# Key weights on ScalarE's DMA queue at the beginning of a one-core decoder kernel

## The chip, the core and the metric

The kernel runs on one core of a Trainium2 chip. A core has a matrix engine (PE, with its weight loads shown apart as PEld), a vector engine (DVE), a scalar engine (ACT), a general engine (POOL), and a sync engine (SP) whose queue issues most of the transfers. The engines run side by side; each takes its own instructions strictly in the order in which they stand in its queue, and waits on semaphores for the others. Transfers between memory and the on-chip buffers are carried by 16 DMA engines. The metric is device time in microseconds (us); less is better.

## The reference, cut to what matters

One decoder layer on 4096 tokens of 512 values: a self-attention without softmax, a cross-attention with softmax on a short context, and a feed-forward block with one shared and 32 routed experts. Only the beginning, the self-attention, is touched by the change:

```
x = residual stream, normalised twice (once before, once in the layer, the second with ln_g and ln_b)
q = x in 4 heads of 128        k = w_fc as 2048 rows of 128 (the same for all tokens)
v = w_proj.T as 2048 rows of 128
out = square(relu(q k^T)) v      x1 = normalised x + residual + out
```

So the keys and values are weights: 512 x 512 numbers each, which are loaded once and serve all tokens and heads.

## The kernel before, in words

**Precision.** Products are made in fp32r with each operand split in a high and a low part. `split` (L89) does it: ACT casts the source to the high part (L94, some calls L96 on DVE), then DVE or POOL subtracts it from the source (L97) to give the low part. A product is then three matrix instructions: high with low, low with high, high with high (`three`, L163). In the profile `kwh`, `kwl` are the parts of the keys (from `wfcT`), `vwh`, `vwl` of the values (from `wpT`), `qh`, `ql` of the queries and `ph`, `pl` of the squared scores. Each weight matrix is four tiles of 128 x 512, 256 KB each. Loads pass through `raw`, a pool of six tiles (L56, L106), so a seventh load waits for the split of the first.

**Stage 0.** `stage0` (L222) goes over tokens in t = 0..7, 512 at a time. `prep(t)` (L231) loads four x tiles (L238), takes their statistics on DVE (L243, L244), a reciprocal root by a power on POOL (L249) and a short chain on DVE (L250 to L254, the last writes `ao`), and writes normalised rows `y` on ACT (L264) or, for two of the four tiles of t = 0, on DVE (L262). Then POOL turns the x tiles into what is added to the attention's output (L273) and SP stores them to `x1` (L274). `prep_head(t, h)` (L278) transposes y for one head on PE (L281), applies gain and bias on ACT (L282) and splits the result.

A step of the main loop (L330) is (t, h, kt): three score products into a bank `s` (L349), relu on ACT into `rl` (L353), square on DVE into `p` or back into the bank (L357), split of p. Seven steps later (`LAG`, L225) `av` (L304) multiplies it with the values into `o` (L311). The score banks alternate between two tags of two buffers each, so that a step needs the bank of the step four before it. There are 512 steps.

**The order of the work.** A planner places the instructions of each engine when the kernel is built, by its own estimate of times and by the order of the code; a program then holds one fixed order for each engine. `g.after(...)` (L73) keeps the instructions in its block behind the named ones on the same engine; `later` (L82) gives a lower priority. All loads and stores of the beginning stand in SP's queue: first the four x tiles, the identity matrix for transposes (L1521), four small stores of an initial list (L1525), gain and bias (L228), then the four tiles of `wfcT` and the four of `wpT` (L107), with mask and zero row between them, and then the weights of the next stage, the stores of `x1` rows and the x tiles of t = 1.

At the beginning, `wfcT` is split behind `g.first`, the normalised rows that DVE writes (L290), the low parts by DVE and POOL in turn; `wpT` is split behind the gain-and-bias step of head 1 (L295), all low parts on DVE; the rows for `x1` follow the last key split (L297), and all four heads of t = 0 are prepared before the loop (L293, L294, L299, L300).

Of the kernel before, what the change touches and what calls it, by code (L numbers as in the profile page):

```python
# [11 lines left out]
I32 = mybir.dt.int32  # L12
# [84 lines left out]
    g.low = (lo_engine or g.nc.vector).tensor_tensor(lo, src, f32(hi), A.subtract)  # L97


def split_steps(g, dram, hi, lo, lo_engine=None):  # L100

    for k in range(len(hi)):
        at = 0
        for h, l in zip(hi[k], lo[k]):
            n = h.shape[-1]
            raw = g.raw.tile([128, n], F32, name="raw", tag="raw")  # L106
            g.nc.sync.dma_start(raw[:], dram[k * 128:(k + 1) * 128, at:at + n])  # L107
            split(g, h, l, raw[:], lo_engine)
            at += n
        if at > 256 or k % 2:  # L110
            yield


def weight_steps(g, dram, nk, width, name, lo_engine=None):
    hi, lo = ([[g.piece(name + z)[:] for _ in range(width // 512)] for _ in range(nk)] for z in "hl")
    yield from split_steps(g, dram, hi, lo, lo_engine)
    return hi, lo


# [99 lines left out]

def stage0(g, x, wfcT, wpT, lnT, x1, background, front):  # L222
    nc = g.nc
    NT = T // 512
    LAG = 7  # L225
    gb = g.c.tile([128, 2, 4], F32, name="gb")
    with later(g, 20):
        nc.sync.dma_start(gb[:], lnT)  # L228
    ys, qs = {}, {}

    def prep(t):  # L231

        rows = [slice(t * 512 + s * 128, t * 512 + s * 128 + 128) for s in range(4)]
        xt = [g.tile("G", "xt") for _ in rows]
        for v, r in zip(xt, rows):
            nc.sync.dma_start(v[:], x[r, :])  # L238
        yield
        mv = g.sm.tile([128, 4, 2], F32, name="am", tag="am")  # L240
        for i, v in enumerate(xt):
            s6 = g.small("as", 6)
            nc.vector.bn_stats(s6[:], v[:])  # L243
            nc.vector.bn_aggr(mv[:, i, :], s6[:])  # L244
            yield
        ve, r0, tt, rs, of = (g.small("a" + z, 8) for z in "vptro")
        nc.vector.tensor_scalar(ve[:, 0:4], mv[:, :, 1], EPS, None, A.add)
        nc.vector.tensor_scalar(ve[:, 4:8], mv[:, :, 1], 1.0 + EPS, EPS * EPS, A.mult, A.add)
        power = nc.gpsimd.tensor_tensor(r0[:], ve[:], g.mhalf[:], A.pow)  # L249
        nc.vector.scalar_tensor_tensor(tt[:], r0[:], -0.5, ve[:], A.mult, A.mult)  # L250
        nc.vector.tensor_tensor(tt[:], tt[:], r0[:], A.mult)
        nc.vector.scalar_tensor_tensor(rs[:], tt[:], 1.5, r0[:], A.add, A.mult)
        mean = mv[:, :, 0].unsqueeze(1).to_broadcast([128, 2, 4])
        nc.vector.scalar_tensor_tensor(of[:].rearrange("p (a n) -> p a n", a=2), mean, -1.0,  # L254
                                       rs[:].rearrange("p (a n) -> p a n", a=2), A.mult, A.mult)
        if t > 0:
            yield
        ys[t] = []
        for i, v in enumerate(xt):
            y = g.tile("C", "y")  # L260
            if t == 0 and i % 2:
                g.first = nc.vector.tensor_scalar(y[:], v[:], mv[:, i, 0:1], rs[:, 4 + i:5 + i], A.subtract, A.mult)  # L262
            else:
                nc.scalar.activation(y[:], v[:], AF.Identity, bias=of[:, 4 + i:5 + i], scale=rs[:, 4 + i:5 + i])  # L264
            ys[t].append(y)
            if i % 2:
                yield

        sc = g.small("bv", 4)
        nc.vector.tensor_scalar(sc[:], rs[:, 0:4], 1.0, None, A.add)  # L270
        for i, v in enumerate(xt):
            with g.after(power):
                nc.gpsimd.tensor_scalar(v[:], v[:], sc[:, i:i + 1], of[:, i:i + 1], A.mult, A.add)  # L273
            nc.sync.dma_start(x1[rows[i], :], v[:])  # L274
            if i % 2:
                yield

    def prep_head(t, h):  # L278
        pt = g.bank("P4", "pt")
        for s in range(4):  # L280
            nc.tensor.transpose(pt[:, s * 128:(s + 1) * 128], ys[t][s][:, h * 128:(h + 1) * 128], g.ident)  # L281
        g.q = nc.scalar.activation(pt[:], pt[:], AF.Identity, bias=gb[:, 1, h:h + 1], scale=gb[:, 0, h:h + 1])  # L282
        qh, ql = g.tile("E", "qh", FR), g.tile("F", "ql", FR)
        split(g, qh[:], ql[:], pt[:])
        qs[t, h] = (qh, ql)

    todo = prep(0)
    while 0 not in ys or len(ys[0]) < 4:
        next(todo)
    with g.after(g.first):  # L290
        kw = run(weight_steps(g, wfcT, 4, 512, "kw", cycle((nc.vector, nc.gpsimd))))
    low = g.low
    prep_head(0, 0)  # L293
    prep_head(0, 1)  # L294
    with g.after(g.q):  # L295
        vw = run(weight_steps(g, wpT, 4, 512, "vw"))
    with g.after(low):  # L297
        run(todo)
    prep_head(0, 2)  # L299
    prep_head(0, 3)  # L300

    P, oT, cur = {}, {}, {}

    def av(t, h, kt):  # L304
        p = P.pop((t, h, kt))
        if kt == 0:
            cur["o"] = g.bank("P3", "o")
        o = cur["o"]
        j, rb = divmod(kt, 4)
        for n, (w, y) in enumerate(three(([part(v, rb, j) for v in vw], p))):  # L310
            nc.tensor.matmul(o[:], w, y[:], start=kt == 0 and n == 0, stop=kt == 15 and n == 2)  # L311
        if kt < 15:
            return
        oT[h] = g.tile("D", "oT")
        nc.scalar.copy(oT[h][:], o[:])
        if h < 3:
            return
        for s in range(4):
            rows = x1[t * 512 + s * 128:t * 512 + s * 128 + 128, :]
            b = g.tile("IJ"[s % 2] if t < NT - 1 else "G", "b")  # L320
            nc.sync.dma_start(b[:], rows)
            pt = g.bank("P4", "pt")
            for hh in range(4):
                nc.tensor.transpose(pt[:, hh * 128:(hh + 1) * 128], oT[hh][:, s * 128:(s + 1) * 128], g.ident)
            nc.vector.tensor_tensor(b[:], pt[:], b[:], A.add)
            nc.sync.dma_start(rows, b[:])

    steps = [(t, h, kt) for t in range(NT) for h in range(4) for kt in range(16)]
    marks = []
    for i, (t, h, kt) in enumerate(steps):  # L330
        if h == 0 and kt == 2 and t + 1 < NT:
            todo = prep(t + 1)
            next(todo)
        if t + 1 == NT and h == 0 and kt == 14:
            todo = front
        if (t + 1 < NT and (h > 0 or kt > 6) or h > 0) and kt % 2:
            with g.after(*marks):
                next(todo, None)
        if (h > 0 if t > 0 else h > 1) and kt % 8 == 6 or t > 0 and h == 0 and kt == 14:
            with g.after(*marks):  # L340
                next(background, None)
        if h > 0 and t + 1 < NT and kt == 12:
            prep_head(t + 1, h - 1)
        if h == 0 and t > 0 and kt == 8:
            prep_head(t, 3)
        s = g.bank(("P1", "P2")[kt % 2], "s")
        j, rb = divmod(kt, 4)
        for n, (w, y) in enumerate(three(([part(k, j, rb) for k in kw], qs[t, h]))):
            nc.tensor.matmul(s[:], w, y[:], start=n == 0, stop=n == 2)  # L349
        if i >= LAG:  # L350
            av(*steps[i - LAG])
        r = g.tile("K", "rl")
        m0 = nc.scalar.activation(r[:], s[:], AF.Relu)  # L353

        apart = i % 8 in (1, 3, 5, 6, 7)
        p = g.tile("H", "p") if apart else s
        m1 = nc.vector.tensor_tensor(p[:], s[:], r[:], A.mult)  # L357
        marks = [m0, m1]
        ph, pl = g.tile("A", "ph", FR), g.tile("B", "pl", FR)
        split(g, ph[:], pl[:], p[:], nc.gpsimd if apart else None, nc.vector if i % 8 == 2 else None)  # L360
        P[t, h, kt] = (ph, pl)
    run(background)
    g.marks = marks
    for st in steps[len(steps) - LAG:]:
        av(*st)
# [1128 lines left out]
def build(tc, I, out):  # L1494
    from contextlib import ExitStack
    nc = tc.nc
    with ExitStack() as outer:
# [15 lines left out]
        with ExitStack() as inner:  # L1513
# [5 lines left out]
            idx = g.c.tile([128, NB], I32, name="idx")  # L1519
            with later(g, 20):  # L1520
                nc.sync.dma_start(ident[:], I["ident"])  # L1521
                empty = g.tile("A", "empty", I32, (128, NBLK))
                nc.gpsimd.memset(empty[:], T)
                for v in lists:
                    nc.sync.dma_start(v[:], empty[:])  # L1525
            g.pairs = Pairs(g, I["sgu"], wS)
            front = {}
            stage0(g, I["x"], I["wfcT"], I["wpT"], I["lnT"], x1,
                   context_steps(g, I["ctxT"], I["wk"], I["wv"], I["wq"], I["wo"], kst, vst),
                   first_rows(g, x1, I["mask"], front))  # L1530
            zero = g.c.tile([128, 4], F32, name="zero")
            nc.gpsimd.memset(zero[:], 0.0)
            nc.sync.dma_start(xs[T:T + 1, :].rearrange("o (p k) -> (o p) k", p=128), zero[:])
# [45 lines left out]
```

## Time and profile before

| | us |
|---|---|
| median of 3 runs | 2693.14 |
| lowest and highest run | 2693.03, 2693.76 |
| profiled execution, its own time | 2691.72 |
| its span, first to last instruction | 2689.9 |
| PE busy | 2631.0 (98%) |
| DVE busy | 2056.8 (76%) |
| ACT busy | 1872.3 (70%) |
| POOL busy | 1205.9 (45%) |

A page of the profile names instructions by line, engine, operation, and `out<-in` by the program's tile names. A timeline row has the start and the length in us, then the instruction, how many of them, and in brackets the engine's idle time before it and what ended that. Windows give each engine's busy time in a stretch. The granted clock of PE is 1.00 in all the windows shown. Of the first 22 us, PE is idle until 11.38, waits until 15.47 for the first product, and until 21.87 for the fifth step's products.

### The profile page before, as it was taken

What the parts mean: (1) busy time and instruction counts of PE and PEld (TensorE: products, weight loads), DVE (VectorE), ACT (ScalarE), POOL (GpSimd) and SP (SyncE); (2) the same over time, 40 slices, a digit from 0 to 9 for tenths busy, and PEclk for the clock granted to TensorE, in tenths of its full rate; (3) what the DMA queues carried; (4) which work ended last, traced back from release to release, by engine and by line L of the source; (5) the groups of instructions that cost most, each with busy time, mean ns of one, the idle gap of its engine ahead of it and who ended that gap; (6) DMA issues with size and microseconds to landing.
All of it is one profiled execution on the core that took longest, in us unless ns stands there. A gap on an engine that the chain in (4) does not pass through costs nothing. (4 is left out here: it accounts for less than half of the span.)

```text
span 2689.9 us, 47615 instructions
## 1 busy us (share of the span) xinstructions
PE 2631.0 (98%) x14592; PEld 2266.3 (84%) x14593; DVE 2056.8 (76%) x4569; ACT 1872.3 (70%) x4155; POOL 1205.9 (45%) x972
## 2 busy tenths in 40 slices
PE   7999999999999999999999998999999999999998
PEld 5888877877789999998988877878989898888886
DVE  7777777777778888898876795674776777778985
ACT  7887787788778777887874332343676767677885
POOL 5765676777654444444446568321122221212221
PEclk9999999999999999999999999999999999999999
DMA  4112112233120324333259656763898899999994
GB/s 154 62 64 95 56 60 91 94 103 104 40 80 18 106 93 136 126 127 126 95 183 365 212 179 202 233 209 111 267 289 275 281 305 293 302 282 290 326 323 140
DMA packets 282289, 463.72 MB, mean 172 GB/s; under 512 B 34512, under 2 KB 85712, under 8 KB 282032
## 3 DMA queue, kind: packets, MB, share of 16 engines
q1 hardware_dynamic: 267344, 433.50, 47.5%
q0 software_dynamic: 14688, 27.17, 4.9%
q8 instruction: 115, 1.88, 0.3%
q14 instruction: 142, 1.16, 0.1%
HBM read 359.58 MB, written 102.93 MB: 172 GB/s over the span
## 5 line engine op out<-in xcount | busy, mean ns | idle before, releaser
L97 DVE TENSOR_TENSOR rl<-raw,rh 128x512 fp32r<-128x512 f32 x768 | 488.8, 685 | 83.7 <-ACT rh L94 58.8
L94 ACT CAST rh<-raw 128x512 fp32r<-128x512 f32 x768 | 437.8, 621 | 135.9 <-DMA raw<-in_rg 85.5
L97 POOL TENSOR_TENSOR pl<-p,ph 128x512 fp32r<-128x512 f32 x320 | 410.8, 1296 | 233.1 <-ACT ph L94 202.8
L353 ACT ACTIVATE rl<-s 128x512 f32<-128x512 f32 x512 | 293.9, 605 | 42.9 <-PE s L349 33.5
L1350 POOL DMA_INDIRECT out_dram<-v,idx x46 | 111.5, 2424 | 461.4 <-ACT v L1348 370.4
L526 POOL TENSOR_TENSOR e<-e,ri 128x512 f32<-128x512 f32 x128 | 133.8, 1051 | 290.1 <-DVE ri L524 147.5
L357 DVE TENSOR_TENSOR p<-s,rl 128x512 f32<-128x512 f32 x320 | 215.1, 683 | 44.5 <-ACT rl L353 38.2
L94 ACT CAST ph<-p 128x512 fp32r<-128x512 f32 x320 | 199.8, 629 | 53.2 <-DVE p L357 51.3
L523 ACT ACTIVATE e<-e,mn 128x128 f32<-128x128 f32 x512 | 199.7, 392 | 25.1 <-DVE mn L518 23.8
L349 PE MATMUL s<-qh,kwl 128*128 128x512 f32 x512 | 206.4, 404 | 10.0 <-DVE p L357 6.7
L1015 PE MATMUL gu<-z,swh 128*128 128x512 f32 x672 | 210.0, 392 | 0.0
L357 DVE TENSOR_TENSOR s<-s,rl 128x512 f32<-128x512 f32 x192 | 133.5, 695 | 98.4 <-ACT rl L353 97.8
L311 PE MATMUL o<-pl,vwh 128*128 128x512 f32 x512 | 203.3, 397 | 1.2 <-POOL pl L97 1.2
L311 PE MATMUL o<-ph,vwl 128*128 128x512 f32 x512 | 200.7, 394 | 0.7 <-ACT ph L94 0.7
L349 PE MATMUL s<-ql,kwh 128*128 128x512 f32 x512 | 200.3, 391 | 0.0
L349 PE MATMUL s<-qh,kwh 128*128 128x512 f32 x512 | 200.2, 391 | 0.0
L311 PE MATMUL o<-ph,vwh 128*128 128x512 f32 x512 | 199.9, 391 | 0.0
L496 PE MATMUL q<-yh,wql 128*128 128x256 f32 x512 | 147.6, 288 | 2.1 <-DVE v L556 1.8
L1015 PEld LDWEIGHTS gu<-z,swh 128*128 128x128 f32 x672 | 126.8, 189 | 25.9
L496 PE MATMUL q<-yh,wqh 128*128 128x256 f32 x512 | 146.4, 286 | 0.0
L496 PE MATMUL q<-yl,wqh 128*128 128x256 f32 x512 | 146.2, 285 | 0.0
L97 DVE TENSOR_TENSOR pl<-s,ph 128x512 fp32r<-128x512 f32 x192 | 131.2, 683 | 16.7 <-ACT ph L94 13.7
(345 smaller groups left out, 7995.5 us busy)
## 6 DMA issues: line engine op xcount, KB each, us to landing
raw<-in_rg SPq DMA_DIRECT2D x256, 256.0 KB, 5.5
raw<-in_ru SPq DMA_DIRECT2D x256, 256.0 KB, 5.3
raw<-in_rd SPq DMA_DIRECT2D x256, 256.0 KB, 4.9
z<-zT SPq DMA_DIRECT2D x112, 256.0 KB, 5.3
raw<-in_sgu SPq DMA_DIRECT2D x48, 256.0 KB, 3.7
swh<-wS SPq DMA_DIRECT2D x48, 256.0 KB, 5.2
swl<-wS SPq DMA_DIRECT2D x48, 256.0 KB, 5.2
xt<-in_x SPq DMA_DIRECT2D x32, 256.0 KB, 3.7
```

What stands on the lines that cost most here:

```text
L94: g.nc.scalar.copy(hi, src)
L97: g.low = (lo_engine or g.nc.vector).tensor_tensor(lo, src, f32(hi), A.subtract)
L311: nc.tensor.matmul(o[:], w, y[:], start=kt == 0 and n == 0, stop=kt == 15 and n == 2)
L349: nc.tensor.matmul(s[:], w, y[:], start=n == 0, stop=n == 2)
L353: m0 = nc.scalar.activation(r[:], s[:], AF.Relu)
L357: m1 = nc.vector.tensor_tensor(p[:], s[:], r[:], A.mult)
L496: nc.tensor.matmul(o[:, i, :], part(w, k, p), y[k // 2][:, k % 2, :], start=n == 0, stop=n == 11)
L523: nc.scalar.activation(e[:, hs], e[:, hs], AF.Exp, bias=mn[:, h:h + 1], scale=-1.0, accum_out=su[:, h:h + 1])
L526: nc.gpsimd.tensor_tensor(e4, e4, ri[:].unsqueeze(2).to_broadcast([128, 4, 128]), A.mult)
L1015: nc.tensor.matmul(o[:], y, z, start=(at, x) not in begun, stop=j == 1 and m == 2, skip_group_check=True)
L1350: nc.gpsimd.indirect_dma_start(out=out, out_offset=bass.IndirectOffsetOnAxis(ap=idx[rows, b + j:b + j + 1], axis=0), in_=v[rows], in_offse ...
```

## The change

The four tiles of `wfcT` are loaded through ACT's queue instead of SP's. Their splits may start behind the statistics (`g.var`, DVE) and behind the power (`g.pow`, POOL) instead of behind the normalised rows. The first two tiles of `wpT` are split there too, the other two behind step 1 of the loop (`run(halves)` at `i == 2`), their low parts by POOL and DVE in turn. The rows for `x1` are made in the loop (steps 3 and 5), head 2 is prepared at step 4 and head 3 at step 8, and the x tiles of t = 1 are asked for at step 6 instead of 2. The four list stores are asked for in `stage0` behind the first two heads.

In the order that the planner makes of it, ACT's queue begins with three loads, the table load, a key cast, the fourth load, three key casts and two value casts, and then the two `y`; the other two value casts stand between the relus of the first steps, as do gain-and-bias of heads 2 and 3. On PE the eight transposes of heads 2 and 3 follow the first four score steps. On DVE two key splits stand between the statistics and the chain that ends with `ao`. On POOL four splits follow the power, then two rows for `x1`, the first `pl`, and the other two rows. On SP the six loads for the next stage come ahead of all stores of `x1`. The number of instructions for the computation is the same.

```diff
-def split_steps(g, dram, hi, lo, lo_engine=None):
+def split_steps(g, dram, hi, lo, lo_engine=None, queue=None):
...
-            g.nc.sync.dma_start(raw[:], dram[k * 128:(k + 1) * 128, at:at + n])
+            (queue or g.nc.sync).dma_start(raw[:], dram[k * 128:(k + 1) * 128, at:at + n])
...
-        nc.vector.tensor_scalar(ve[:, 4:8], mv[:, :, 1], 1.0 + EPS, EPS * EPS, A.mult, A.add)
-        power = nc.gpsimd.tensor_tensor(r0[:], ve[:], g.mhalf[:], A.pow)
+        g.var = nc.vector.tensor_scalar(ve[:, 4:8], mv[:, :, 1], 1.0 + EPS, EPS * EPS, A.mult, A.add)
+        power = g.pow = nc.gpsimd.tensor_tensor(r0[:], ve[:], g.mhalf[:], A.pow)
...
-    with g.after(g.first):
-        kw = run(weight_steps(g, wfcT, 4, 512, "kw", cycle((nc.vector, nc.gpsimd))))
-    low = g.low
+    with g.after(g.var, g.pow):
+        kw = run(weight_steps(g, wfcT, 4, 512, "kw", cycle((nc.vector, nc.gpsimd)), nc.scalar))
+    vw = tuple([[g.piece("vw" + z)[:]] for _ in range(4)] for z in "hl")
+    halves = split_steps(g, wpT, *vw, cycle((nc.gpsimd, nc.vector)))
+    with g.after(g.var, g.pow):
+        next(halves)
+        next(halves)
     prep_head(0, 0)
     prep_head(0, 1)
-    with g.after(g.q):
-        vw = run(weight_steps(g, wpT, 4, 512, "vw"))
-    with g.after(low):
-        run(todo)
-    prep_head(0, 2)
-    prep_head(0, 3)
+    empty = g.tile("A", "empty", I32, (128, NBLK))
+    nc.gpsimd.memset(empty[:], T)
+    for v in lists:
+        nc.sync.dma_start(v[:], empty[:])
...
-        if h == 0 and kt == 2 and t + 1 < NT:
+        if i == 2:
+            with g.after(*marks):
+                run(halves)
+        if t == h == 0 and kt in (3, 5):
+            with g.after(*marks):
+                next(todo)
+        if h == 0 and kt == (2 if t > 0 else 6) and t + 1 < NT:
...
-        if h == 0 and t > 0 and kt == 8:
+        if i == 4:
+            prep_head(0, 2)
+        if h == 0 and kt == 8:
             prep_head(t, 3)
```

More of the change, by code (lines that the diff above doesn't have):

```diff
@@ L111, in split_steps, with weight_steps @@
             yield
-def weight_steps(g, dram, nk, width, name, lo_engine=None):
+def weight_steps(g, dram, nk, width, name, lo_engine=None, queue=None):
     hi, lo = ([[g.piece(name + z)[:] for _ in range(width // 512)] for _ in range(nk)] for z in "hl")
-    yield from split_steps(g, dram, hi, lo, lo_engine)
+    yield from split_steps(g, dram, hi, lo, lo_engine, queue)
     return hi, lo
@@ L218, in context_steps, with stage0 @@
     g.wo2 = yield from weight_steps(g, wo, 8, 512, "wo", pool)
-def stage0(g, x, wfcT, wpT, lnT, x1, background, front):
+def stage0(g, x, wfcT, wpT, lnT, x1, background, front, lists):
     nc = g.nc
@@ L261, in prep @@
             if t == 0 and i % 2:
-                g.first = nc.vector.tensor_scalar(y[:], v[:], mv[:, i, 0:1], rs[:, 4 + i:5 + i], A.subtract, A.mult)
+                nc.vector.tensor_scalar(y[:], v[:], mv[:, i, 0:1], rs[:, 4 + i:5 + i], A.subtract, A.mult)
             else:
@@ L1521, in build @@
                 nc.sync.dma_start(ident[:], I["ident"])
[L1522 to L1525, printed above, removed]
             g.pairs = Pairs(g, I["sgu"], wS)
@@ L1529, in build @@
                    context_steps(g, I["ctxT"], I["wk"], I["wv"], I["wq"], I["wo"], kst, vst),
-                   first_rows(g, x1, I["mask"], front))
+                   first_rows(g, x1, I["mask"], front), lists)
             zero = g.c.tile([128, 4], F32, name="zero")
```

## The prediction

> **What bounds the kernel now.** I read the page's first two parts first, for the bound of the whole.
>
> ```profile
> span 2689.9 us, 47615 instructions
> PE 2631.0 (98%) x14592; PEld 2266.3 (84%) x14593; DVE 2056.8 (76%) x4569; ACT 1872.3 (70%) x4155; POOL 1205.9 (45%) x972
> ...
> PE   7999999999999999999999998999999999999998
> ```
>
> PE is busy in 98% of the span and only the first slice is short (7). The change adds no matrix product and takes none away, so it can move the time only by PE's idle time at the beginning. In the built programs every engine's order differs only at the start: the last 14,587 of PE's 14,643 instructions, and all but the first 20 to 35 entries of ACT, DVE and POOL, stand in the same order before and after. So I follow the start up to the point where the orders meet again. The windows tell how much there is to gain:
>
> ```profile
> 2.30:6.00 3.70, 0.00 (x0) 0.00 (x0) 2.38 (x6) 0.00 (x0) 0.00 (x0) 1.00 0.97 323
> 9.00:13.50 4.50, 1.97 (x8) 1.57 (x8) 2.64 (x9) 3.50 (x6) 0.88 (x1) 1.00 1.03 341
> 16.00:22.00 6.00, 5.06 (x21) 3.94 (x20) 5.18 (x9) 5.33 (x10) 4.53 (x4) 1.00 0.88 272
> 22.00:32.00 10.00, 10.00 (x42) 7.49 (x43) 9.01 (x16) 8.51 (x18) 6.03 (x5) 1.00 0.91 307
> 32.00:40.00 8.00, 8.00 (x37) 6.63 (x36) 7.88 (x16) 5.70 (x11) 3.72 (x4) 1.00 0.02 4
> ```
>
> (Stretch, length, busy time of PE, PE's weight loads, DVE, ACT, POOL, clock, DMA share, GB/s.) From 22 us on PE doesn't idle. Before that the DMA engines are full twice: at 0.97 while x arrives, at 1.03 while wfcT and wpT arrive. The timeline then gives the chain that leads to PE's first work:
>
> ```profile
> 5.84 0.69 DVE L243 BATCH_NORM_STATS2 as<-xt 128x6 f32<-128x512 f32 x1
> 7.18 1.67 POOL L249 TENSOR_TENSOR ap<-av,mhalf 128x8 f32<-128x8 f32 x1 [6.21 <-DVE av L248]
> 9.49 0.17 DVE L254 SCALAR_TENSOR_TENSOR ao<-am,ar 128x8 f32<-128x8 f32 x1
> 9.99 0.62 ACT L94 CAST kwh<-raw 128x512 fp32r<-128x512 f32 x1 [8.00 <-DMA raw<-in_wfcT]
> 10.52 1.51 ACT L264 ACTIVATE y<-xt,ao,ar 128x512 f32<-128x512 f32 x2
> 11.38 1.97 PE L281 MATMUL pt<-ident,y 128*128 128x128 f32 x8 [11.38 <-ACT y L264]
> 13.64 0.61 ACT L94 CAST kwh<-raw 128x512 fp32r<-128x512 f32 x1
> 15.47 2.07 PE L349 MATMUL s<-qh,kwl 128*128 128x512 f32 x4 [2.12 <-ACT qh L94]
> 21.87 0.47 PE L349 MATMUL s<-qh,kwl 128*128 128x512 f32 x1 [0.94 <-DVE p L357]
> ```
>
> The reader sees three limits in turn: the fourth x tile (its statistics start at 5.84), then ACT's casts of wfcT in front of and between its own y, pt and qh work, then at 21.87 PE waiting for DVE's p, because the score banks are used up after four steps. I count score steps of t=0, h=0 from 0.
>
> **The change part by part.**
>
> *Loading wfcT from ACT.* Three of the four loads are issued by ACT ahead of its table load (1.28 us, at 0.71 before), the fourth behind the first cast. The four list stores (0.43 us of SP each) leave the front of SP's queue. One issue costs SP 0.43 us and I take the same for ACT: 1.3 us and the table load end by about 3.4, before any weight lands, so ACT loses nothing. The bytes do cost. The row: from 2.3 to 6.0 us the DMA engines are at 0.97 with x from SP alone, 323 GB/s. [...] Read by the issue order alone, x would land at 5.74 as before. [...] I take 2.2: the fourth x tile lands at 7.9. Bounds: 5.8 (SP's rows first) and 8.8 (the fourth wfcT tile ahead too). With the first, the y would be ready at 9.7, but see wpT below.
>
> *The chain behind x.* From x landing to ao is 9.66 - 5.74 = 3.92 us. DVE now has two kwl splits inside it (0.69 each), under POOL's 1.67 us power; they fit, and cost 0 to 0.9 if POOL's activity stretches them (a kwl split beside a POOL split took 1.35). I take 0. ao is ready at 11.8.
>
> *ACT ahead of y.* ACT now has four kwh casts and two vwh casts (0.52 apart) queued in front of y. Each waits for its load. In the built program a DMA also waits for the earlier user of its completion semaphore, eight taken in turn over both queues: ident waits for the first wfcT tile, the two wpT loads for the second x and the second wfcT tile, so they leave at about 5.8 and 6.2. Their bytes are through by about 10; with the 5.3 us to landing that wpT took before, 11.5. A cast later is 10.7 or 12.1, against y ready at 11.8: cost 0 to 0.3. I take 0. So y starts at 11.85, where it started at 10.52: 1.33 later, of which 0.86 had been ACT's cast in the way.
>
> *From y to the first product.* The first transpose follows 0.86 behind y (12.7), the sixth ends at 14.2; then pt, pt, qh without casts between: 14.25, 14.9, 15.57 to 16.17. First product at 16.2 instead of 15.47: 0.73 later. This is where the early split pays: 0.6 us of cast between the two pt are gone.
>
> *Heads 2 and 3 moved behind the first products.* PE no longer has four transposes (0.85 us) inside the first score block. From the first product to the first finished score is 2.85 us (before 3.63 less 0.85), so rl of step 0 starts at 19.05; I call it A. ACT's queue from A, one every 0.5 us, pt 0.66: rl0 0, rl1 0.7, vwh 1.2, ph0 1.7, rl2 2.25, vwh 2.75, ph1 3.3, rl3 3.8, pt 4.3, pt 4.95, rl4 5.6, qh 6.1, ph3 6.6, rl5 7.1, qh 7.6, ph4 8.1. What was done before the loop (two vwh casts, one pt, one qh) now stands in it. DVE: p0 0.65, p1 1.35 to 2.05, pl0 to 3.05, p2 to 3.7, vwl to 4.45, ph2 to 5.1, p3 to 5.75. POOL: vwl 1.9 to 3.2, two x1 rows (L273) to 5.7, pl1 to 7.0, two rows to 8.8, pl3 to 10.1; a row took 0.77 to 2.26 in the timeline:
>
> ```profile
> 15.58 4.95 POOL L273 TENSOR_SCALAR xt<-xt,bv,ao 128x512 f32<-128x512 f32 x4
> 23.31 1.30 POOL L97 TENSOR_TENSOR pl<-p,ph 128x512 fp32r<-128x512 f32 x1 [2.78 <-ACT ph L94]
> ```
>
> Before, these rows were over at 20.5, ahead of the first pl; now they stand between pl1 and pl3, at 1.0 us each. PE goes on at A+2.3 (21.35, where it was 21.87: 0.5 earlier), runs ten products, waits for p3 from 4.55 to 5.8 (1.25 us: step 7 needs step 3's bank), and waits for pl3 until A+10.15 (0.9 us). That product, PE's 54th entry in both orders, is at 19.05 + 10.15 = 29.2; before it was at 28.29. After it PE never idled up to 43.8, so nothing there takes 0.9 back; at the stalls of 43.8 and 51.8 (0.37 and 1.21 us) ACT is the one that is late, and it is itself 0.5 later, so at most 0.4 can be regained.
>
> *The x1 stores and the next x tiles.* These four stores now stand behind all six wk loads on SP, the last two of which wait for POOL's and DVE's vwl (A+3.2, A+4.5). First store at 24.1, landed 2.5 later, the x tile that takes its buffer 3 later: 29.6. DVE's statistics on it are due at A+10.4 = 29.5, in order, with the p products behind them. Cost 0 to 4.5; 0 taken, as by then only eight transfers share 6 us.
>
> *The lists.* 0.43 us x 4 of SP, now at 7.3 to 9.1 where SP only waits; nothing reads them until much later. Nothing.
>
> **Sum.** +0.73 (first product) - 1.25 (fewer transposes and casts up to the first p) + 1.25 (p3) + 0.9 (pl3), less 0.7 us of small gaps that PE had before between 21.87 and 28.29: about +0.9 us on a span of 2689.9, so 2690.8. The profiled run took 2691.7, 1.8 more than its span, and the median of the runs is 1.4 above that, 2693.1. Forecast 2694.0. What a measurement can tell from no change is about 0.2%, 5.4 us; this is no change.
>
> **The rivals.**
>
> *The gain is kept (chance 0.2).* SP's rows go first and x lands near 5.8; then y waits for wpT's casts, to 10.7, first product 15.05, and 54th entry at 28.05 even with both stalls. If POOL's rows run at 0.77 the second stall halves. That is 0.3 to 2 us faster, 2691 to 2692.8. For it: 0.86 us of cast do leave the chain. Against it: the DMA share of 0.97. PE can't resume before x, chain, transposes and four steps are through, so over 5.4 us faster has 0.05 at most, and only by something that I don't see.
>
> *The next x tiles come late (0.16): slower.* The place is DVE's statistics at 29.5. If store and load take what they took in the full stretch before (3.8 and 6.1 us), the tile lands at 24.1 + 9.9 = 34.0, DVE stops for 4.5 us with p7 behind it, and PE's bank wait follows: +0.9 + 4.5 = 5.4 us, 2698.5; with x at 8.8 in the first place, 2699.4. It decides from a landing at about 34. Against it: the DMA engines had 22 transfers in that stretch before and have about half now.
>
> *Nothing moves (0.15).* The stalls at 43.8 and 51.8 us swallow the difference: 2693.1.
>
> **How the numbers follow.** The likeliest, 0.9 slower, has 0.49 with its costs' bounds from -0.3 (x early) to +3.3 (x at 8.8, splits stretched 0.9, POOL's rows at 2.26): 2692.8 to 2696.4. The range of eight in ten reaches into both neighbours: 2690.5 to 2699.0. Faster by over 0.2%: 0.05. Slower: most of the late-tile case and a little of unseen, 0.16. Within: 0.79.
>
> **What would show it.** Right: the fourth statistics at about 8 us, y at 11.9, first score product near 16.2; a wait of PE on p of about 1.2 us and one on POOL's pl of about 0.9 before 30 us; full PE after it. Wrong: statistics ending by 6.6 (queues don't share), DVE waiting for x at 29 us or later for over 1 us, or a difference that arises behind 45 us, where the order is the same.

## The result, and the profile after

| | before | after |
|---|---|---|
| median, us | 2693.51 (22 runs, 2691.58 to 2698.60) | 2698.03 (22 runs, 2695.06 to 2701.89) |
| profiled execution, its own time, us | 2691.72 | 2698.08 |
| its span, us | 2689.9 | 2696.3 |

The change made the kernel slower by 4.5 us: the ratio of the medians is 1.0017, with a 95% interval from 1.0011 to 1.0023. So the sign is clear of the noise, though the size is still under the 5.4 us that the prediction took as the least that can be told. The forecast was 2694.0, that is 0.9 slower; the measured time lies inside its range, near the upper end.

The first two parts of the page of after answer to those of before: the same work, and the first slice one tenth emptier.

```profile
span 2696.3 us, 47613 instructions
PE 2631.8 (98%) x14593; PEld 2265.3 (84%) x14593; DVE 2057.7 (76%) x4567; ACT 1873.9 (69%) x4155; POOL 1206.3 (45%) x974
...
PE   6999999999999999999999998999999999999998
```

The windows of after, in the same stretches as those shown of before, with its window from 6 to 9 us beside them (stretch, length, busy time of PE, PE's weight loads, DVE, ACT, POOL, clock, DMA share, GB/s):

```profile
2.30:6.00 3.70, 0.00 (x0) 0.00 (x0) 1.22 (x3) 1.89 (x3) 0.00 (x0) 1.00 0.99 336
6.00:9.00 3.00, 0.00 (x0) 0.00 (x0) 2.03 (x6) 1.07 (x2) 0.00 (x0) 1.00 1.07 385
9.00:13.50 4.50, 0.00 (x0) 0.00 (x0) 3.47 (x7) 1.85 (x3) 3.92 (x3) 1.00 0.71 180
16.00:22.00 6.00, 4.04 (x13) 3.26 (x14) 2.26 (x4) 3.42 (x6) 0.00 (x0) 1.00 0.44 147
22.00:32.00 10.00, 9.95 (x41) 7.48 (x40) 7.73 (x14) 8.85 (x18) 6.44 (x7) 1.00 0.29 105
32.00:40.00 8.00, 7.61 (x34) 5.97 (x33) 7.12 (x14) 5.67 (x12) 5.87 (x5) 1.00 0.94 328
```

Up to 9 us the DMA engines are full (0.99 and 1.07) with x and the key weights together. From 9 to 13.5 us, where PE did its first transposes before (1.97 us), it now does nothing, and POOL is busy for 3.92 us instead of 0.88. From 22 us on PE is almost full again. The timeline of after gives the chain in between:

```profile
8.27 0.66 DVE L243 BATCH_NORM_STATS2 as<-xt 128x6 f32<-128x512 f32 x1
9.33 1.29 DVE L97 TENSOR_TENSOR kwl<-raw,kwh 128x512 fp32r<-128x512 f32 x2
9.57 1.97 POOL L249 TENSOR_TENSOR ap<-av,mhalf 128x8 f32<-128x8 f32 x1 [8.60 <-DVE av L248]
11.53 2.47 POOL L97 TENSOR_TENSOR kwl<-raw,kwh 128x512 fp32r<-128x512 f32 x2
11.58 1.23 DVE L250 SCALAR_TENSOR_TENSOR at<-ap,av 128x8 f32<-128x8 f32 x1 [0.96 <-POOL ap L249]
12.85 1.19 DVE L251 TENSOR_TENSOR at<-at,ap 128x8 f32<-128x8 f32 x1
13.97 1.25 POOL L97 TENSOR_TENSOR vwl<-raw,vwh 128x512 fp32r<-128x512 f32 x1
14.07 1.19 DVE L252 SCALAR_TENSOR_TENSOR ar<-at,ap 128x8 f32<-128x8 f32 x1
15.29 0.17 DVE L254 SCALAR_TENSOR_TENSOR ao<-am,ar 128x8 f32<-128x8 f32 x1
15.49 1.52 ACT L264 ACTIVATE y<-xt,ao,ar 128x512 f32<-128x512 f32 x2 [4.43 <-DVE ao L254]
19.93 2.08 PE L359 MATMUL s<-qh,kwl 128*128 128x512 f32 x4 [1.60 <-ACT qh L94]
```

Two things are later than before. The fourth x tile's statistics start at 8.27 instead of 5.84. And three instructions of DVE on 128 x 8 numbers, L250, L251 and L252, take 1.23, 1.19 and 1.19 us, where each took 0.17, as the timeline of before shows:

```profile
8.89 0.17 DVE L250 SCALAR_TENSOR_TENSOR at<-ap,av 128x8 f32<-128x8 f32 x1 [1.86 <-POOL ap L249]
9.09 0.17 DVE L251 TENSOR_TENSOR at<-at,ap 128x8 f32<-128x8 f32 x1
9.29 0.17 DVE L252 SCALAR_TENSOR_TENSOR ar<-at,ap 128x8 f32<-128x8 f32 x1
```

In after, each ends with the POOL instruction beside it: the first split of POOL's pair from 11.53 is over at 12.78 and L250 at 12.81; the pair is over at 14.00 and L251 at 14.04; POOL's third is over at 15.22 and L252 at 15.26.

Step by step, as differences between the two profiles (the entries of PE are its matrix instructions, counted from the first):

| | before | after | difference |
|---|---|---|---|
| fourth statistics start | 5.84 | 8.27 | +2.43 |
| length of the power (POOL L249) | 1.67 | 1.97 | +0.30 |
| end of the power to end of ao | 0.80 | 3.91 | +3.11 |
| end of ao to ACT's y | 0.86 | 0.03 | -0.83 |
| start of ACT's y | 10.52 | 15.49 | +4.97 |
| first product | 15.47 | 19.93 | +4.46 |
| fifth step's products | 21.87 | 26.00 | +4.13 |
| PE's 57th entry | 28.97 | 33.60 | +4.63 |
| ACT's first y of t = 1 | 47.05 | 52.00 | +4.95 |

The 54th entry of PE, on which the prediction's sum ends, is not the same instruction in both orders: the last product of the stall in after (`o<-pl,vwh`, 32.80), a score product in before (28.29). From the 57th on the orders agree.

From the y of t = 1 on, the same ACT instruction is 4.94 us later at 87 us, 4.91 at 208 us, and 4.65 at 694 us. I call the value at about 87 us the settled shift of a kernel. It is what the beginning costs, and it agrees with the 4.5 us between the medians. It is known to about 0.3 us: near 240 us eight of the ten changed kernels step down by 0.3 against before, and two don't. The profiles' spans differ by 6.4; the rest of that arises behind 780 us, where the order of the instructions is the same.

### The profile page after: what moved, and what is told of

It reads as the page before. It is cut to its first block, busy times and chain, and to the rows that moved or that the text cites. A ratio compares the mean times of both kernels' runs of the same rounds, so it can differ in the third digit from the quotient of the medians.

```text
span 2696.3 us, 47613 instructions
## 1 busy us (share of the span) xinstructions
PE 2631.8 (98%) x14593; PEld 2265.3 (84%) x14593; DVE 2057.7 (76%) x4567; ACT 1873.9 (69%) x4155; POOL 1206.3 (45%) x974
## 5 line engine op out<-in xcount | busy, mean ns | idle before, releaser
L97 DVE TENSOR_TENSOR pl<-s,ph 128x512 fp32r<-128x512 f32 x192 | 131.2, 683 | 16.3 <-ACT ph L94 13.5
```

## The experiments

The theory after the result: the chain from the power to `ao` stood still because POOL's splits ran beside it (3.1 us and 0.3 in the power), and the queue made x late (2.4 us). The rivals: only the queue counts; or the heads, stalls and late x tiles behind the first product, which the prediction had weighed, make the loss. Runs of one kernel lie up to 7 us apart (before: 2691.58 to 2698.60), and ten or twenty of them leave the median open by a microsecond or two, so I compare the kernels by the steps in their traces, with the medians beside them. Each trace is one execution; each ratio is to runs of before made beside that kernel.

| kernel | fourth statistics | power's end to ao's end | y | first product | fifth step | settled shift | median (runs) | ratio to before, 95% |
|---|---|---|---|---|---|---|---|---|
| before | 5.84 | 0.80 | 10.52 | 15.47 | 21.87 | 0 | 2693.51 (22) | |
| after | 8.27 | 3.91 | 15.49 | 19.93 | 26.00 | +4.94 | 2698.03 (22) | 1.0017, 1.0011 to 1.0023 |
| queue only | 8.72 | 0.80 | 12.57 | 17.52 | 23.92 | +2.21 | 2695.85 (12) | 1.0003, 0.9994 to 1.0012 |
| POOL beside | 7.30 | 2.37 | 12.72 | 17.99 | 24.39 | +2.37 | 2696.46 (12) | 1.0007, 0.9998 to 1.0015 |
| POOL behind ao | 8.11 | 0.80 | 12.27 | 17.22 | 22.92 | +2.30 | 2694.80 (12) | 1.0004, 0.9995 to 1.0013 |
| keys on SP | 6.16 | 4.75 | 13.96 | 18.40 | 23.74 | +3.55 | 2698.01 (20) | 1.0012, 1.0006 to 1.0019 |
| both undone | 5.86 | 0.80 | 9.72 | 14.67 | 20.41 | +0.27 | 2692.65 (11) | 0.9996, 0.9987 to 1.0005 |
| x on two queues | 6.34 | 0.80 | 10.57 | 15.52 | 22.06 | +0.37 | 2693.45 (11) | 0.9997, 0.9988 to 1.0006 |
| heads first | 8.11 | 0.80 | 12.26 | 17.21 | 23.62 | +3.98 | 2695.50 (10) | 1.0003, 0.9994 to 1.0013 |
| lists behind | 6.07 | 0.80 | 9.92 | 14.87 | 21.44 | -0.19 | 2692.23 (11) | 0.9992, 0.9983 to 1.0001 |
| own x buffers | 6.47 | 0.81 | 10.32 | 15.27 | 20.41 | -0.12 | 2690.78 (11) | 0.9991, 0.9982 to 1.0000 |

### The queue alone

Before, with nothing but the key loads through ACT's queue:

```diff
-        kw = run(weight_steps(g, wfcT, 4, 512, "kw", cycle((nc.vector, nc.gpsimd))))
+        kw = run(weight_steps(g, wfcT, 4, 512, "kw", cycle((nc.vector, nc.gpsimd)), nc.scalar))
```

> The kernel before with one part of the change alone: wfcT is loaded through ACT's queue, all else as before. Theory (two causes: x shares the DMA engines with wfcT, and POOL's splits hold up DVE's short chain): only the first cause is there. The fourth x tile's statistics start near 8.3 us as in the changed kernel (before 5.84), the chain from L250 to L254 stays at 0.8 us, y on ACT starts near 12.1 (before 10.52), the first score product near 17.1 (before 15.47), about +1.6 us in all. Rival (sharing costs nothing because wfcT would have been in the way anyway): statistics later, but first product within 0.3 us of 15.47.

Its timeline, the fourth statistics and the chain's first instruction:

```profile
8.72 0.69 DVE L243 BATCH_NORM_STATS2 as<-xt 128x6 f32<-128x512 f32 x1
11.77 0.17 DVE L250 SCALAR_TENSOR_TENSOR at<-ap,av 128x8 f32<-128x8 f32 x1 [1.86 <-POOL ap L249]
```

With the key loads on ACT's queue the DMA share is 0.98 from 2.3 to 6 us and 1.00 from 6 to 9, where before has 0.97 and 0.69, and x alone becomes late: by 2.88 us, more than in after itself. The chain stays at 0.17 an instruction. ACT's y comes only 2.05 later, because 0.83 of that was ACT's cast, which no longer stands in the way. The settled shift is +2.21 where about 1.6 was expected. So the queue makes less than half of the loss (2.21 of 4.94).

### POOL's work beside the chain

Before, with three subtractions of POOL on 128 x 512 numbers put behind the power of t = 0. They work on a scratch tile and nobody reads them.

```diff
+        if t == 0:
+            du = g.tile("B", "du")
+            nc.gpsimd.memset(du[:], 0.0)
+            with g.after(power):
+                for _ in range(3):
+                    nc.gpsimd.tensor_tensor(du[:], du[:], du[:], A.subtract)
         nc.vector.scalar_tensor_tensor(tt[:], r0[:], -0.5, ve[:], A.mult, A.mult)
```

> The kernel before with three additional 128x512 POOL operations on a scratch tile right behind the power, and nothing else changed; x lands as before (statistics at 5.84). Theory (a POOL operation on large tiles holds up DVE's short operations): each of L250, L251, L252 takes about 1.2 us instead of 0.17, ao is ready near 12.8 instead of 9.66, y on ACT starts near 12.8 (before 10.52), first product near 17.7, about +2.3 us in all. Rival (the short DVE operations were slow in the changed kernel for the transfers landing beside them, or for the order on DVE): L250 to L252 stay at 0.17 us and the time stays within 0.3 us.

The timeline of this kernel:

```profile
10.30 3.29 POOL L255 TENSOR_TENSOR du<-du 128x512 f32<-128x512 f32 x3
10.35 1.01 DVE L256 SCALAR_TENSOR_TENSOR at<-ap,av 128x8 f32<-128x8 f32 x1 [1.87 <-POOL ap L249]
11.39 0.17 DVE L257 TENSOR_TENSOR at<-at,ap 128x8 f32<-128x8 f32 x1
11.59 0.90 DVE L258 SCALAR_TENSOR_TENSOR ar<-at,ap 128x8 f32<-128x8 f32 x1
12.52 0.17 DVE L260 SCALAR_TENSOR_TENSOR ao<-am,ar 128x8 f32<-128x8 f32 x1
12.60 1.01 DVE L276 TENSOR_SCALAR bv<-ar 128x4 f32<-128x4 f32 x1
```

POOL's work on a scratch tile does it too: L256 is held for 1.01 us and L258 for 0.90, where before has 0.17. The expectation is met in part. The second instruction slipped in between two of POOL's and took 0.17, so the chain grew by 1.57 and not by three whole lengths. And x landed 1.5 us late in this run though its loads are those of before. The arithmetic of y still closes: 1.46 (x) + 1.57 (chain) - 0.83 (the cast is out of the way) = 2.20, and y moved from 10.52 to 12.72.

### POOL's work behind the chain

After, with one small instruction of POOL that reads `ao` and whose result nobody reads. The splits stand behind it instead of behind the power.

```diff
+        if t == 0:
+            gt = g.small("gt", 8)
+            g.gate = nc.gpsimd.tensor_scalar(gt[:], of[:], 1.0, None, A.add)
...
-    with g.after(g.var, g.pow):
+    with g.after(g.var, g.gate):
         kw = run(weight_steps(g, wfcT, 4, 512, "kw", cycle((nc.vector, nc.gpsimd)), nc.scalar))
...
-    with g.after(g.var, g.pow):
+    with g.after(g.var, g.gate):
         next(halves)
         next(halves)
```

> The changed kernel with POOL's early splits held behind ao by a 128x8 POOL operation that reads ao; the loads stay as in the change. Theory: L250 to L254 take 0.8 us instead of 3.9, y starts near 12.3 instead of 15.49, first product near 16.8 instead of 19.93; about 3.1 us less than the changed kernel, so +1.4 against before. Rival (the moved work in the loop is what costs): y earlier, but the products from the fifth step on less than 1 us earlier than in the changed kernel.

Its timeline:

```profile
9.46 1.97 POOL L249 TENSOR_TENSOR ap<-av,mhalf 128x8 f32<-128x8 f32 x1 [8.48 <-DVE av L248]
11.46 0.17 DVE L250 SCALAR_TENSOR_TENSOR at<-ap,av 128x8 f32<-128x8 f32 x1 [1.57 <-POOL ap L249]
11.66 0.17 DVE L251 TENSOR_TENSOR at<-at,ap 128x8 f32<-128x8 f32 x1
11.86 0.17 DVE L252 SCALAR_TENSOR_TENSOR ar<-at,ap 128x8 f32<-128x8 f32 x1
12.33 0.46 POOL L258 TENSOR_SCALAR gt<-ao 128x8 f32<-128x8 f32 x1 [0.90 <-DVE ao L254]
12.78 1.50 POOL L97 TENSOR_TENSOR kwl<-raw,kwh 128x512 fp32r<-128x512 f32 x1
```

All three are back at 0.17, and the settled shift falls from +4.94 to +2.30. The medians point the same way: the ratio to before falls from 1.0017 to 1.0004. Nothing else of the change was undone, so to have POOL's splits beside the chain costs 2.64 us (of which 0.16 is x, which landed that much earlier here). That is less than the 3.1 expected, since from y to the first product it takes 4.95 us again instead of 4.44. The power is still 1.97, as in after: in both a key split of DVE had begun a quarter of a microsecond before it.

### The keys back on SP, and both undone

After without the queue:

```diff
-        kw = run(weight_steps(g, wfcT, 4, 512, "kw", cycle((nc.vector, nc.gpsimd)), nc.scalar))
+        kw = run(weight_steps(g, wfcT, 4, 512, "kw", cycle((nc.vector, nc.gpsimd))))
```

> The changed kernel with wfcT loaded through SP's queue again, behind x, identity and gain and bias; all else as in the change. Theory: statistics of the fourth x tile at 5.84 again, but POOL's splits still run beside L250 to L254 and one DVE split stands in the chain, so ao near 13, y near 13 instead of 15.49; 2.4 us less than the changed kernel, so about +2 against before. Rival (the queue is the whole cause): back to 2693.5 or below.

x comes early again (6.16), but only 1.39 us of the shift go, and +3.55 are left, more than expected. The timeline says why: the chain now takes 4.75 us, since a key split of DVE has come to stand inside it and is itself held beside POOL.

```profile
9.54 2.94 POOL L97 TENSOR_TENSOR kwl<-raw,kwh 128x512 fp32r<-128x512 f32 x2 [0.37 <-ACT kwh L94]
10.18 1.18 DVE L97 TENSOR_TENSOR kwl<-raw,kwh 128x512 fp32r<-128x512 f32 x1 [0.59 <-ACT kwh L94]
11.28 1.22 DVE L251 TENSOR_TENSOR at<-at,ap 128x8 f32<-128x8 f32 x1
12.54 1.19 DVE L252 SCALAR_TENSOR_TENSOR ar<-at,ap 128x8 f32<-128x8 f32 x1
```

The two causes therefore don't simply add: with x early, the keys and POOL's splits meet the chain in another order. The last edit and this one together, that is, the key weights back on SP and POOL's splits behind `ao`:

> The changed kernel with both causes taken away: wfcT through SP's queue behind x, identity and gain and bias, and POOL's early splits held behind ao. Theory: statistics of the fourth x tile near 6 us, L250 to L254 in 0.8 us, y on ACT near 9.8, first product near 14.7 (before 15.47), and from there to the 54th product 12.9 us as in all the runs so far: 27.6 against 28.29, so 0.5 to 0.9 us faster than before. Rival (the moved heads, value splits and x1 rows cost something of their own): first product as said, 54th product later than 28.3.

y is at 9.72, 0.80 earlier than before, and the fifth step at 20.41, 1.46 earlier. PE's 54th entry is at 27.57, as expected (27.6), and its 57th 0.59 earlier than in before. But the settled shift is +0.27: the gain of 0.5 to 0.9 us that was expected is gone. The waits of DVE from 25 to 60 us name what can have taken it back:

```profile
DVE as L243 <- DMA xt<-in_x: 1.9, 3, 0.9
```

These are the statistics of t = 1, 1.9 us in three waits for x tiles: the late tiles that the prediction had as a rival. A tile of t = 1 can be loaded only when the `x1` row in its buffer is stored, and these stores stand behind six loads on SP.

### The x tiles of t = 0 in buffers of their own

The last kernel, with the four x tiles of t = 0 in another pool's buffers, so that the tiles of t = 1 needn't wait for the stores:

```diff
-        xt = [g.tile("G", "xt") for _ in rows]
+        xt = [g.W.tile([128, 512], F32, name="x0", tag="W") if t == 0 else g.tile("G", "xt") for _ in rows]
```

> The kernel of e5 with the x tiles of t=0 in buffers of their own, so that the loads of the x tiles of t=1 need not wait for the x1 stores; PE's, ACT's and DVE's orders are those of e5. Against the kernel before, e5's ACT instructions ran 1.0 us early at 26.7 us and 0.3 us late from 40 us on. Theory (e5 loses its lead to DVE, which waits for the late x tiles of t=1): no wait of DVE for x behind 25 us, and the lead of about 1.0 us stays from 40 us on, about 2692.4. Rival (the lead is lost on ACT or POOL, which have the moved work to catch up with): no lead from 40 us on, as in e5.

In its waits of DVE from 25 to 60 us no x tile appears any more; two lines are left:

```profile
DVE s L370 <- ACT rl L366: 3.5, 3, 1.6
DVE p L370 <- ACT rl L366: 1.8, 3, 1.2
```

The expectation, that the lead of 1.0 us which ACT had at 26.7 us in "both undone" would stay, failed: the settled shift is -0.12. In this profile x landed 0.6 us later than in the kernel before it (statistics at 6.47), for the same loads, so the first product leads by 0.20 and not by 0.80. And the lead at 26.7 us was no lasting one: PE's stall on POOL's pl (0.55 us in both kernels, in front of the 54th entry) takes a part of it. Measured from PE's 57th entry, where that stall is over, to the settled value, "both undone" loses 0.86 us (-0.59 to +0.27), and this kernel 0.10 (-0.22 to -0.12). Of the 0.86, 0.57 goes between PE's 87th and 99th entry, behind the wait of 0.81 us for the third x tile at 34.34. The other 0.27 goes near the 120th, where "queue only", whose DVE doesn't wait for x, loses 0.3 too. So the late tiles explain 0.6 to 0.8 us of what was given back. The median is 2690.78 against 2693.55 beside it, ratio 0.9991 with an interval from 0.9982 to 1.0000. It is the lowest of all versions, at the edge of what can be told from no change.

### x on two queues

"Both undone", with the second and fourth x tile of t = 0 through ACT's queue:

```diff
-            nc.sync.dma_start(v[:], x[r, :])
+            (nc.scalar if t == 0 and r.start % 256 else nc.sync).dma_start(v[:], x[r, :])
```

> The same as the one above, with the second and fourth x tile loaded through ACT's queue. Theory (two queues share the DMA engines, only issue time is saved): the fourth tile's statistics come within 0.5 us of those of the one-queue kernel, all else the same, no difference of time that can be told. Rival (the second queue brings bandwidth of its own): statistics near 4.8 us, 1 us faster.

The fourth statistics start at 6.34 instead of 5.86, the first at 4.40 instead of 3.34. So a second queue didn't bring x any faster here.

### Heads 2 and 3 before the loop again

"POOL behind ao", with heads 2 and 3 prepared ahead of the first products as in before:

```diff
     prep_head(0, 1)
+    prep_head(0, 2)
+    prep_head(0, 3)
...
-        if i == 4:
-            prep_head(0, 2)
-        if h == 0 and kt == 8:
+        if h == 0 and t > 0 and kt == 8:
```

> The changed kernel with POOL's early splits held behind ao, and heads 2 and 3 prepared ahead of the loop again. Against the kernel with only the splits held (54th product at 30.09, first product at 17.22): theory (the move of the heads neither costs nor brings anything, as its work is only shifted on ACT): first product within 0.3 us of 17.2, 100th product within 0.5 us of 44.5. Rival from the prediction (the moved heads save 1.25 us to the fifth step and then pay 2.15 us in two stalls): PE's fifth step later by 1 us and the 100th product earlier by 1 us.

Both expectations failed. The settled shift is +3.98 instead of +2.30, so by the two traces moving the heads behind the first products saves 1.68 us; the medians don't show it (ratios of 1.0003 and 1.0004). 0.70 of it is there at the fifth step (23.62 instead of 22.92). The rest comes behind it and before PE's 57th entry, where the waits of PE up to 60 us show two stalls:

```profile
PE o L318 <- POOL pl L97: 1.2, 1, 1.2
PE s L362 <- DVE pl L97: 0.9, 2, 0.6
```

### The list stores alone

Before, with only the four list stores, and the tile that they store, moved behind the weight loads:

```diff
-                empty = g.tile("A", "empty", I32, (128, NBLK))
-                nc.gpsimd.memset(empty[:], T)
-                for v in lists:
-                    nc.sync.dma_start(v[:], empty[:])
...
     prep_head(0, 3)
+    empty = g.tile("A", "empty", I32, (128, NBLK))
+    nc.gpsimd.memset(empty[:], T)
+    for v in lists:
+        nc.sync.dma_start(v[:], empty[:])
```

> The kernel before with one part of the change alone: the four list stores stand behind the weight loads on SP. Theory: wfcT lands about 2 us earlier (first cast on ACT near 7.8 instead of 9.99), so that cast leaves the gap in front of y: y on ACT near 9.8 instead of 10.52, first product 0.7 us earlier than 15.47, 0.7 us faster than before in all. Rival (x is the limit and the cast fitted anyway): no difference.

The fifth step comes 0.43 us earlier and the settled shift is -0.19. The key weights leave SP 1.9 us earlier (at 3.53 instead of 5.44), so ACT's first cast is out of the way of y. y comes 0.60 earlier and the first product too, somewhat less than the 0.7 expected; x landed 0.23 later in this profile. The ratio is 0.9992, from 0.9983 to 1.0001: a gain that can't be told from none by its runs, and that the prediction had put at nothing.

## Why the prediction was right in sign and too small

The sign and most steps came as forecast. That the time lies inside the range is luck: the likeliest case, with all the bounds of its costs, ended at 2696.4, and the range went on to 2699.0 for x tiles of t = 1 that come late, at a cost of 4.5 us. They cost 0.3 us at most. What brought the time to 2698.03 is a term that the prediction put at nothing, the hold of the chain behind x.

**The bound, and where to look: right.** PE's idle time at the beginning sets what the change is worth. The settled shift of 4.94 us is all there before 90 us.

**Loading wfcT from ACT: right.** The prediction weighed the issue order (5.74) against the DMA share of 0.97 and took 2.2 us, an estimate of its author. No run shows the 2.2 as such; the runs showed the fourth statistics 2.43 later in after (8.27, where about 8 was forecast) and 2.88 with the queue alone.

**The chain behind x: this step failed.** It read "they fit, and cost 0 to 0.9 if POOL's activity stretches them ... I take 0", and looked only at the two splits of DVE that were new in the chain. Those did fit under the power, and cost 0.30 by making the power longer. What was lost is that POOL's own new splits, which the text listed on POOL's queue, start at the very moment at which the chain goes on. The chain's instructions were costed at their length in a place where POOL was idle. The end of the power to the end of ao grew by 3.11 us, three and a half times the bound. "POOL beside" shows that POOL's work alone does it, and "POOL behind ao" that taking it away brings 2.64 us back.

The row that says so was in the trace of before: the same three instructions for t = 1, where POOL makes low parts beside them. The timeline of before:

```profile
42.32 2.53 POOL L97 TENSOR_TENSOR pl<-p,ph 128x512 fp32r<-128x512 f32 x2
43.02 0.61 DVE L250 SCALAR_TENSOR_TENSOR at<-ap,av 128x8 f32<-128x8 f32 x1
44.16 0.71 DVE L251 TENSOR_TENSOR at<-at,ap 128x8 f32<-128x8 f32 x1
45.03 1.29 POOL L97 TENSOR_TENSOR pl<-p,ph 128x512 fp32r<-128x512 f32 x1 [0.17 <-ACT ph L94]
45.40 0.94 DVE L252 SCALAR_TENSOR_TENSOR ar<-at,ap 128x8 f32<-128x8 f32 x1
```

0.61, 0.71 and 0.94 us where the start has 0.17 three times; L251 ends at 44.87 with POOL's pair at 44.85, L252 at 46.34 with POOL's third at 46.32. So by this row an instruction of the chain ends with the POOL instruction beside it, and the sum would have had the chain behind three POOL splits of 1.25 us each, an estimate of about 3.1 us more. With the 0.3 by which the power grew, which is known only from the runs, the forecast would have been 2694.0 + 3.1 + 0.3 = 2697.4.

**ACT ahead of y: right.** The cast that stood in front of y is gone: ao to y went from 0.86 to 0.03.

**From y to the first product: right.** 4.35 us were forecast (11.85 to 16.2); it took 4.44, where it was 4.95. Splitting early pays this half microsecond.

**From the first product to PE's 54th entry: right in sum.** 13.0 us were forecast (16.2 to 29.2), and it took 12.87. The parts differ: to the fifth step 6.07 instead of 5.15, and from there 6.80 instead of 7.85, with a stall of 0.2 us on p and 0.55 on POOL's pl instead of 1.25 and 0.9. The timeline of PE in after shows the first miss:

```profile
24.36 0.63 PE L359 MATMUL s<-ql,kwh 128*128 128x512 f32 x1
24.79 0.59 PE L359 MATMUL s<-qh,kwh 128*128 128x512 f32 x1
25.21 1.04 PE L281 MATMUL pt<-ident,y 128*128 128x128 f32 x8
26.00 0.48 PE L359 MATMUL s<-qh,kwl 128*128 128x512 f32 x1
26.32 0.40 PE L359 MATMUL s<-ql,kwh 128*128 128x512 f32 x1
```

All twelve first products are 0.43 us apart, where in before they are 0.23 apart from 18.9 us on; the eight transposes fill the time to 26.00, and PE itself was not ready sooner. I take PE's clock for the cause. The 1.00 that the windows print up to here is no measurement: the trace's first record of the granted clock, a full one, begins at 25.20 us in after and at 18.80 in before, and what lies ahead of it counts as full. Where a half clock is on record (0.50 from 1800.6 to 1804.0 us in before), products are 0.43 us apart too, and 0.23 behind it. The record begins at a different distance from the first product in each trace. The six kernels that move the heads behind the first products show what that does (us; the stall on p is the time between two starts on PE beyond 0.23):

| kernel | first product to full clock | first product to fifth step | stall on p | first product to 54th entry |
|---|---|---|---|---|
| own x buffers | 3.19 | 5.14 | 0.94 | 12.68 |
| keys on SP | 3.64 | 5.34 | 0.91 | 12.89 |
| POOL behind ao | 4.45 | 5.70 | 0.58 | 12.87 |
| both undone | 4.53 | 5.74 | 0.52 | 12.90 |
| after | 5.27 | 6.07 | 0.21 | 12.87 |
| x on two queues | 6.23 | 6.54 | 0 | 12.89 |

With an early full clock the forecast 5.15 and most of the stall on p come out; with a late one PE reaches the fifth step later and waits for p by so much less. At the 54th entry, 12.7 to 12.9 us behind the first product in all six, nothing of it is left. The heads by themselves, which the sum did not cost alone, are worth 1.68 us in "heads first".

**The next x tiles: there, but small.** DVE waits once for an x tile of t = 1, for 0.9 us up to 34.07, where the rival had 4.5. ACT's shift grows from +4.64 to +4.98 behind it; PE stands at +4.64 until its 117th entry, and at +4.95 from the 123rd on, near the stall of 43.8 us of before, where the prediction hoped to regain up to 0.4. That the wait makes this step is not shown, since "queue only" has a step of 0.3 there without such a wait.

**The lists: 0.2 to 0.4 better than the nothing taken.** **The rivals:** the kept gain needed x near 5.8, and fell with the fourth statistics at 8.27; the unmoved time needed the stalls at 43.8 and 51.8 to swallow the difference, and the shift grew near the first.

In one sum: of the 4.0 us by which +4.94 exceeds the +0.9, 3.1 are the chain and 0.3 the power; the fourth statistics came some 0.3 later than forecast, and 0.3 came near 48 us.

What stays open: why the rest of the profiles' spans differs by another 1.5 us behind 780 us, where the instructions stand in the same order. Other traces wander there too, either way: from 780 us to the end "queue only" goes from +2.0 to +6.0 and "POOL behind ao" from +2.2 to -0.6. A part of that goes with the clock: near 1.8 ms a half clock is on record for 3.41 us in before, for 6.83 in "queue only" and not at all in "POOL behind ao", and from 1800 to 1900 us their shifts change by +1.1 and -1.2. After has the same 3.41 as before, so its 1.5 us are not that. Open too is why the medians of five kernels (POOL behind ao, both undone, heads first, lists behind, own x buffers) lie 1.0 to 2.7 us below what their settled shifts would give.

## What to carry to other kernels

Before work is put on POOL beside a chain of short DVE instructions, look for the same instructions elsewhere in the trace where POOL is busy: in after a 0.17 us step on 128 x 8 numbers took 1.19 to 1.23 us beside POOL splits of 1.25, and three of them in a row cost 3.1. Loads that needn't be early can, from an idle queue, delay the one load that the start waits for: in after the key loads were issued from 0.71 us on, on ACT's queue, instead of from 5.44 on SP's, and the fourth x tile's statistics came 2.43 us later (2.88 in "queue only"); x itself on two queues came no earlier (6.34 instead of 5.86). Where the medians scatter by more than the effect, the shift of one and the same instruction behind the changed stretch can tell kernels apart that their medians can't; but a trace is one execution, and what its loads happened to do is in the shift.

## What the runs showed of the hardware that was not expected

- A short DVE instruction with two inputs of 128 x 8 numbers was over only when the POOL split or subtraction beside it was: it took 0.90 to 1.23 us instead of 0.17, in after and in "POOL beside" five times, each ending 0.02 to 0.04 us behind POOL's. One that came between two POOL instructions took 0.17. L276 in "POOL beside", with 128 x 4 numbers of one input, was held as well (1.01 us instead of 0.16).
- It goes the other way round too, by the order of the starts. POOL's power took 1.97 to 2.08 us where a split of DVE had begun before it (after, POOL behind ao, x on two queues, heads first), and each time it ended 1.54 us behind that split. It took 1.67 or 1.68 where none ran beside it (before, queue only, POOL beside) or one began after it (keys on SP, both undone, own x buffers).
- The power does not hold DVE's split. A split of DVE that began while the power ran took its usual 0.69 us in four kernels (after at 9.93, keys on SP at 8.83, both undone at 7.27, own x buffers at 8.53). It is why the two splits did fit under the power. Beside a POOL split, DVE's took longer (1.18 us in keys on SP); why the one holds it and the other doesn't is open.
- The record of PE's full clock began 2.98 us (POOL beside) to 6.23 us (x on two queues) behind the first product, in after 5.27, and in each of the eleven traces the products change from 0.43 to 0.23 us apart there. So the point lay up to 3.25 us apart from one trace to another.
- x landed at different times for the same loads: the fourth statistics started between 5.84 and 7.30 us in the kernels with x alone at the front of SP's queue. So a step read from one profile of a start is good to about half a microsecond, and once (POOL beside) it was 1.5 off.
